# A two-layer gated attention kernel on one core: the first weights centred on TensorE, the first inputs prepared ahead, five staging buffers

## The chip, the cores and the metric

One Trainium2 (trn2) chip, one core. The metric is the device time of one execution in microseconds, as the median over runs. PE is TensorE (PEld its weight loads), DVE VectorE, ACT ScalarE, POOL GpSimd, SP the queue that issues most transfers. A transfer is issued by an engine's queue in its program order; every engine runs its instructions in order and waits where an operand isn't ready.

## The reference

A residual stream x of 16 batches x 128 tokens x 256 passes four blocks; the first is the one around which the change lies:

```python
x = x + tanh(g_xattn[0]) * L0_xattn(layernorm(x), ctx, ...)
x = x + tanh(g_ffn[0])   * L0_ffn(layernorm(x), ...)
x = x + tanh(g_xattn[1]) * L1_xattn(layernorm(x), ctx, ctx, ...)
x = x + tanh(g_ffn[1])   * L1_ffn(layernorm(x), ...)

# L0_xattn: 16 heads of 128, 8 key/value groups
ln_out = _ln(hidden_states, ln_w, ln_b)
q  = _ln(_fp8_linear_pertensor(ln_out, wq, wq_scale, q_in_scale).reshape(b, s, g, hpg, d), qln_w, qln_b)
k  = _ln(_fp8_linear_pertensor(ln_out, wk, wk_scale, k_in_scale).reshape(b, s, g, d), kln_w, kln_b)
v  = _fp8_linear_pertensor(ln_out, wv, wv_scale, v_in_scale).reshape(b, s, g, d)
core = _gqa(q, k, v)
qx = _ln(_fp8_linear_pertensor(ln_out, wqx, ...), qxln_w, qxln_b)
kx, vx = split(cond @ w_kv_x.T);  kx = _ln(kx, kxln_w, kxln_b)
xout = _gqa(qx, kx, vx)
cat = concatenate([core, xout]);  catq = _div_clamp_fp8(cat, proj_smooth)
return einsum(catq, wproj) * (proj_in_scale * proj_w_scale)
```

Queries and keys are layer-normalised over the 128 elements of a head. The mean that this subtracts can be taken out of the weights instead: when each head's 128 output columns of the weight matrix have zero mean (per input row), the projected head has zero mean. This is called centring here.

## The kernel before

The first block is 32 units: units 0 to 15 are one batch each of self-attention, units 16 to 31 one batch each of cross-attention. A unit goes through: preparation of its input (`prep_norm` subtracts and scales on DVE to xh; `prep_tr` transposes on PE and applies ln_w, ln_b on DVE to lnT; `prep_scale` multiplies on POOL to in_y; `prep_round` clamps and rounds on DVE; `prep_last` ends the rounding on POOL to xs and xx, and writes xx to memory, xqx), projection in eight blocks of 512 columns (L431: K 0 and 1, Q 2 to 5, V 6 and 7), eviction on ACT to raw or vt (L443, L440), statistics on DVE (`bn`, L452), a reciprocal root (q_r, L312), its multiplication into raw on POOL (`mult`, L475), transposes of the heads (L486) with eviction on ACT to kT, qT (L495), scores (L504), maximum on DVE (mx, L512), exponentials on ACT (L520), division on POOL (L532), transposes (L540), values (L550), smoothing and rounding to cat (L561, L237), and the output product (L591).

The loop runs over steps n from -11; a unit takes four steps, and at each step `do` and `once` call the stages of several units at their lags, so that stages of different units interleave. `front` gives the two projection blocks of a step: unit u is projected from n = 4u - 5. The order of the calls gives priorities; a scheduler with a cost model of its own settles the order on each engine.

The weights are loaded in the same loop, by `loads`: keys and queries at n = -8, -6 and -5, values at -4, projection weights (`load_proj`, wproj) at -2 and -1. `load_split` loads a 128x512 tile into a staging buffer (`stage`, three buffers), centres it for K and Q (`center`: a reduce and a scaling on DVE, L212 and L213, a subtraction on POOL, L214), and splits it into a rounded part on ACT (L202) and the rest on DVE (L203). `load_proj` splits without centring (L199, L200). `stats` loads four batches of x (xg) and takes their statistics. `load_kv1` loads small weights of the third block (ak, av) and a tile of ctx, and `kv1` (L640, L644) uses them. The weights for the cross half come into the same staging buffers at n around 56 to 60 (`load_kvx`, `load_split` with K_QX).

Where the input preparation stands in a step, before: 

```python
            once(n, -6, "prep_last")
...
            once(n, -8, "prep_norm")
            once(n, -8, "prep_tr")
            once(n, -7, "prep_scale")
            once(n, -7, "prep_round")
```

Of the kernel before, what the change touches and what calls it, by code (L numbers as in the profile page):

```python
# [9 lines left out]
F32 = mybir.dt.float32  # L10
# [5 lines left out]
ALU = mybir.AluOpType  # L16
AX = mybir.AxisListType

P = 128
B = 16  # L20
DM = 256
# [10 lines left out]
K_Q, K_K, K_V, K_QX = 0, 1, 2, 3  # L32
# [3 lines left out]
def flamingo_kernel(  # L36
# [27 lines left out]
    nc = tc.nc  # L64
# [6 lines left out]
    const = ctx.enter_context(tc.tile_pool(name="const", bufs=1))  # L71
# [11 lines left out]
    def ps_tr(shape):  # L83
        return ps("tr", shape, 2)
# [17 lines left out]
    def stay_after(ins, other):  # L102

        tc.add_manual_dep(
            ins.ins, other.ins.name,
            mybir.DependencyInfo(
                mybir.DependencyClass.NoSync, mybir.DependencyReason.DATA
            ),
            reason="the other is awaited",
        )  # L110

    def kpn(ap):
        return ap.rearrange("(k p) n -> p k n", p=P)
# [7 lines left out]
    ident = const.tile([P, P], F32, name="ident")  # L121
# [45 lines left out]
    NST = 512  # L167
# [39 lines left out]
    def center(st, dst):  # L207

        nh = NST // P
        sh = st.rearrange("p (h d) -> p h d", d=P)  # L210
        mean = small.tile([P, nh], F32, tag="wmean", name="wmean")
        nc.vector.tensor_reduce(mean, sh, AX.X, ALU.add)  # L212
        nc.vector.tensor_scalar(mean, mean, 1.0 / P, None, ALU.mult)  # L213
        nc.gpsimd.tensor_tensor(  # L214
            dst.rearrange("p (h d) -> p h d", d=P), sh,
            mean[:, :, None].to_broadcast([P, nh, P]), ALU.subtract,
        )

    def e4m3(dsts, y, pool):


        n = y.shape[1]
        e = pool.tile([P, n], BF16, tag="e8_e", name="e8_e")
        t = pool.tile([P, n], BF16, tag="e8_t", name="e8_t")
        nc.vector.tensor_scalar(y, y, FP8_MAX, -FP8_MAX, ALU.min, ALU.max)
        nc.vector.tensor_scalar(
            e.bitcast(U16), y.bitcast(U16), 0x7F80, None, ALU.bitwise_and
        )

        nc.vector.tensor_scalar(e, e, 2.0**-6, 24.0, ALU.max, ALU.mult)  # L230
        nc.vector.tensor_tensor(t, y, e, ALU.add)  # L231

        def last(other=None):
            at = 0
            for dst in dsts:
                part = slice(at, at + dst.shape[1])
                ins = nc.gpsimd.tensor_tensor(dst, t[:, part], e[:, part], ALU.subtract)  # L237
                if other is not None:
                    stay_after(ins, other)
                at += dst.shape[1]  # L240

        return last
# [11 lines left out]
    with (  # L254
# [3 lines left out]

        wt = {}
        wpr = {}  # L260

        def load_split(kind, src, c):

            for k in range(KD):
                st = ap.tile([P, NST], F32, tag="stage", name="stage", bufs=3)
                nc.sync.dma_start(
                    out=st, in_=src[k * P : (k + 1) * P, c * NST : (c + 1) * NST]
                )
                scale = wsc[:, 2 * kind + k : 2 * kind + k + 1]
                if kind != K_V:  # L270
                    center(st, st)
                slot = "q" if kind == K_QX else "qkv"[kind]
                hi, lo = (
                    (xp if i and slot != "q" else wp).tile(
                        [P, NST], F32R, tag=f"w{slot}{i}{k}{c}", name=f"w{slot}{i}{k}{c}"
                    )
                    for i in range(2)
                )
                split(st, scale, hi, lo)
                wt[kind, 0, k, c], wt[kind, 1, k, c] = hi, lo  # L280
# [11 lines left out]
        def load_proj(cross, q):  # L292

            n = NST // DM
            dst = wp.tile([P, 4, 2, DM], F32R, tag=f"wp{q}", name=f"wp{q}")
            for c in range(0, 4, n):
                h0 = 16 * cross + 4 * q + c
                st = ap.tile([P, n, DM], F32, tag="stage", name="stage", bufs=3)
                nc.sync.dma_start(out=st, in_=kpn(wprojT)[:, h0 : h0 + n, :])
                split(st, None, dst[:, c : c + n, 0, :], dst[:, c : c + n, 1, :])  # L300
            wpr[cross, q] = dst
# [15 lines left out]
        def stats(g):  # L317

            xg = ap.tile([P, 4, DM], F32, tag="xg", name="xg", bufs=1)
            nc.sync.dma_start(  # L320
                out=xg, in_=x_in[4 * g : 4 * g + 4].rearrange("b s d -> s b d")
            )
            mv = small.tile([P, 4, 2], F32, tag="mv0", name="mv0", bufs=2)
            for j in range(4):
                stx = small.tile([P, 6], F32, tag="st0", name="st0")
                nc.vector.bn_stats(stx, xg[:, j, :])
                nc.vector.bn_aggr(mv[:, j, :], stx)

            v = small.tile([P, 4], F32, tag="v1", name="v1", bufs=1)
            nc.vector.tensor_scalar(v, mv[:, :, 1], 1.0 + EPS, EPS * EPS, ALU.mult, ALU.add)  # L330
            rr = rsqrt0(v, 4, "x")
            for j in range(4):
                norms[4 * g + j] = (xg[:, j, :], mv[:, j, 0:1], rr[:, j : j + 1])
# [278 lines left out]
        units = [Unit(u) for u in range(NU)]  # L612
# [3 lines left out]
        av = ap.tile([P, KD, NG * HD], F32, tag="av", name="av", bufs=1)  # L616
        cxs = {}
# [2 lines left out]
        kv1_at[4 * (B - 1) + 1] = B - 1  # L620

        def load_kv1(b):
            if b == 0:
                for k in range(KD):
                    nc.sync.dma_start(
                        out=ak[:, k].rearrange("p (g d) -> p g d", d=HD),
                        in_=akT[k * P : (k + 1) * P, :].rearrange(
                            "p (g h d) -> p g h d", h=NH // NG, d=HD
                        )[:, :, 0, :],
                    )  # L630
                nc.sync.dma_start(out=av, in_=kpn(avT))
            cxs[b] = ap.tile([P, KD, P], F32, tag="ctx", name="ctx")
            nc.sync.dma_start(out=cxs[b], in_=kpn(ctxT)[:, :, b * P : (b + 1) * P])

        def kv1(b):
            cx = cxs.pop(b)
# [42 lines left out]
        def once(n, step, name, *args):  # L679

            m = n - step
            if m % 4 == 0 and 0 <= m // 4 < NU:
                getattr(units[m // 4], name)(*args)
# [7 lines left out]
        first, last = -11, 4 * NU + 7  # L691
        for n in range(first, last + 1):
            for m in range(0, B, 4):
                if n == 4 * m - 11:
                    stats(m // 4)
            once(n, -8, "load")
            for f, args in loads.get(n, ()):
                f(*args)
            ab = [front(n, i) for i in range(2)]
            do(n, 1, "recip")  # L700
            do(n, 4, "quant_last")
            do(n, 1, "divide")
            do(n, 0, "scores")
            do(n, 2, "probs")
            do(n, 0, "top")
            do(n, 0, "exp")
            if ab[0]:
                ab[0][0].project(ab[0][1])
                ab[0][0].evict(ab[0][1])
            once(n, -6, "prep_last")  # L710
            do(n, 3, "values")
            do(n, 3, "smooth")
            if ab[0]:
                ab[0][0].bn(ab[0][1])
            once(n, -2, "rstd")
            for blk in range(2):
                once(n, -2, "mult", blk)
                once(n, -1, "heads", blk)
            do(n, -2, "mult_q")
            do(n, -1, "heads_q")  # L720
            do(n, 3, "quant")
            if ab[1]:
                ab[1][0].project(ab[1][1])
                ab[1][0].evict(ab[1][1])
                ab[1][0].bn(ab[1][1])
            if n + 4 in kv1_at:
                load_kv1(kv1_at[n + 4])
            if n in kv1_at:
                kv1(kv1_at[n])
            do(n, 5, "output")  # L730
            once(n, 8, "residual")
            once(n, -8, "prep_norm")
            once(n, -8, "prep_tr")
            once(n, -7, "prep_scale")
            once(n, -7, "prep_round")

    G = 4
    NT = G * P
# [85 lines left out]
    for j in range(B):  # L824
# [9 lines left out]
        out=before, in_=ones, pattern=[[1, P]], compare_op=ALU.is_gt, fill=0.0,  # L834
# [20 lines left out]
    def route(b0, G):  # L855
# [88 lines left out]
        out=causal, in_=causal, pattern=[[-1, P]], compare_op=ALU.is_ge, fill=NEG,  # L944
# [5 lines left out]
    for q in range(P // 32):  # L950
# [3 lines left out]
            out=rows, in_=rows, pattern=[[-HD, NQ]], compare_op=ALU.is_ge, fill=0.0,  # L954
# [3 lines left out]
            out=rows, in_=rows, pattern=[[HD, NQ]], compare_op=ALU.is_ge, fill=0.0,  # L958
# [223 lines left out]
    ap = f2.enter_context(tc.tile_pool(name="a1", bufs=2, side="right", reuse_waits="tile"))  # L1182
# [171 lines left out]
```

## Time and profile before

| | us |
|---|---|
| median of 3 runs | 1501.8 (1501.51 to 1504.62) |
| profiled execution, its own time | 1503.01 |
| its span | 1501.3 |
| PE busy | 1369.6 (91%) |
| DVE busy | 988.6 (66%) |
| ACT busy | 838.4 (56%) |
| POOL busy | 687.6 (46%) |
| unit 0's first projection (L431) starts | 26.54 |
| unit 1's | 50.6 |
| unit 2's | 76.0 |

Times in the profile count from the span's start. A line of the timeline has the start, the time taken, the engine, the line of the kernel, the operation, output and input, and in brackets how long the engine stood idle before and what ended that. The clock column (PEclk) is the share of TensorE's full speed that was granted. A matmul of float32 operands is two instructions in the trace.

### The profile page before, as it was taken

Reading aid. Unit: us, or ns where it says so; the run is one execution under the profiler, and the core shown is the slowest. Engines: PE = TensorE matmul, PEld = TensorE weight load, DVE = VectorE, ACT = ScalarE, POOL = GpSimd, SP = SyncE. Lnnn points to the kernel's source line nnn. Section 1 sums busy time; section 2 is a strip of 40 time slices with the busy share of each in tenths; the row PEclk is TensorE's granted clock in tenths of the full one; section 3 lists DMA queues with packets and bytes.
Section 4 is the critical chain, followed back from the end, with each engine's and each line's share of the span. In section 5 each row is a group of like instructions: output and inputs, shape, how many; then the busy total and the mean of one; then the engine's idle time right before and its main releaser. Section 6 shows DMA issues by size and latency. Waiting matters only on the chain. (4 is left out here: it accounts for less than half of the span.)

```text
span 1501.3 us, 21652 instructions
## 1 busy us (share of the span) xinstructions
PE 1369.6 (91%) x6852; PEld 964.4 (64%) x6852; DVE 988.6 (66%) x2597; ACT 838.4 (56%) x2496; POOL 687.6 (46%) x615
## 2 busy tenths in 40 slices
PE   2789899899988999999999997999999999985998
PEld 1578778687776777777777766555544444444887
DVE  7867878778689777777676764453478787762100
ACT  3666566666656676666666663164476575741221
POOL 4476677677766565656556563121032322111111
PEclk9699999999999999999999998899999999986999
DMA  4300101000013100000000000700042212122652
GB/s 133 110 17 23 38 22 38 21 22 27 22 55 104 45 29 19 15 16 17 12 18 15 15 4 27 211 8 14 31 128 53 75 50 63 40 75 76 196 189 70
DMA packets 78770, 80.37 MB, mean 54 GB/s; under 512 B 15291, under 2 KB 64891, under 8 KB 78656
## 3 DMA queue, kind: packets, MB, share of 16 engines
q1 hardware_dynamic: 65152, 55.29, 12.7%
q10 hardware_dynamic: 11456, 17.63, 3.6%
q0 software_dynamic: 2048, 6.07, 1.1%
q8 instruction: 55, 0.90, 0.3%
q14 instruction: 59, 0.48, 0.1%
HBM read 57.14 MB, written 22.05 MB: 53 GB/s over the span
## 5 line engine op out<-in xcount | busy, mean ns | idle before, releaser
L532 POOL TENSOR_TENSOR e<-e,sums 128x512 f32<-128x512 f32 x128 | 141.4, 1105 | 239.7 <-DVE sums L528 100.8
L475 POOL TENSOR_TENSOR raw<-raw,q_r 128x512 f32<-128x512 f32 x192 | 211.3, 1126 | 21.0 <-DVE q_r L312 19.6
L520 ACT ACTIVATE e<-ps_sc,mx 128x128 f32<-128x128 f32 x512 | 181.1, 368 | 63.6 <-DVE mx L512 58.1
L452 DVE BATCH_NORM_STATS2 q_st<-raw 128x6 f32<-128x128 f32 x768 | 174.2, 279 | 64.2 <-ACT raw L443 63.6
L591 PE MATMUL ps_acc<-wp,cat 128*128 128x512 f32 x512 | 159.3, 433 | 14.0 <-POOL cat L237 13.4
L504 PE MATMUL ps_sc<-kT,qT 128*128 128x128 f32 x1024 | 140.9, 281 | 23.9 <-ACT qT L495 23.9
L542 ACT COPY eT<-ps_tr 128x512 f32<-128x512 f32 x128 | 75.3, 588 | 156.3 <-PE ps_tr L540 156.3
L504 PEld LDWEIGHTS ps_sc<-kT,qT 128*128 128x128 f32 x1024 | 132.4, 194 | 44.1 <-ACT qT L495 36.6
L237 POOL TENSOR_TENSOR cat<-e_t,e_e 128x1024 fp32r<-128x1024 bf16 x64 | 136.6, 2135 | 43.5 <-DVE e_t L231 43.5
L1082 ACT ACTIVATE e<-ps_sc,mx 128x128 f32<-128x128 f32 x512 | 139.0, 392 | 30.5 <-DVE mx L1073 30.1
L550 PE MATMUL ps_pv<-eT,vt 128*128 128x256 f32 x512 | 133.8, 383 | 1.0 <-DVE cat_y L561 1.0
L443 ACT COPY raw<-ps_mm 128x512 f32<-128x512 f32 x192 | 113.8, 593 | 29.2 <-PE ps_mm L431 25.8
L591 PEld LDWEIGHTS ps_acc<-wp,cat 128*128 128x128 f32 x512 | 94.6, 191 | 53.4 <-POOL cat L237 20.1
L486 PE MATMUL ps_tr<-ident,raw 128*128 128x128 f32 x768 | 115.2, 276 | 13.6 <-POOL raw L475 11.6
L486 PEld LDWEIGHTS ps_tr<-ident,raw 128*128 128x128 f32 x768 | 91.6, 141 | 47.5 <-POOL raw L475 20.5
L561 DVE TENSOR_TENSOR cat_y<-ps_pv,r_sm 128x512 bf16<-128x512 f32 x128 | 87.1, 680 | 47.2 <-PE ps_pv L550 46.7
L550 PEld LDWEIGHTS ps_pv<-eT,vt 128*128 128x128 f32 x512 | 97.3, 192 | 30.9 <-issue 10.5
L512 DVE TENSOR_REDUCE mx<-ps_sc 128x4 f32<-128x512 f32 x128 | 87.2, 682 | 38.5 <-PE ps_sc L504 37.8
L495 ACT ACTIVATE qT<-ps_tr,hv 128x512 f32<-128x512 f32 x128 | 101.2, 791 | 19.9 <-PE ps_tr L486 17.7
L520 ACT ACTIVATION_READ_ACCUMULATOR e<-ps_sc,mx 128x1 f32 x512 | 105.4, 206 | 0.0
L1093 PEld LDWEIGHTS ps_tr<-ident,e 128*128 128x128 f32 x512 | 59.9, 142 | 64.9 <-ACT e L1082 28.1
L1073 DVE TENSOR_REDUCE mx<-ps_sc 128x8 f32<-128x1024 f32 x64 | 77.6, 1212 | 30.2 <-PE ps_sc L1066 20.9
(221 smaller groups left out, 2687.0 us busy)
## 6 DMA issues: line engine op xcount, KB each, us to landing
w1t<-in_w ACTq DMA_DIRECT2D x8, 1024.0 KB
w2t<-in_w ACTq DMA_DIRECT2D x8, 1024.0 KB
disp<-empty SPq DMA_DIRECT2D x16, 257.0 KB
xe<-disp SPq DMA_DIRECT2D x8, 514.0 KB
ctx<-in_ctxT SPq DMA_DIRECT2D x32, 128.0 KB
stage<-in_wprojT SPq DMA_DIRECT2D x16, 256.0 KB
ods<-og SPq DMA_DIRECT2D x128, 32.0 KB
ov<-ods SPq DMA_DIRECT2D x32, 128.0 KB
```

Source lines behind the costliest of these rows:

```text
L237: ins = nc.gpsimd.tensor_tensor(dst, t[:, part], e[:, part], ALU.subtract)
L443: nc.scalar.copy(raw.rearrange("p h d -> p (h d)"), pm)
L452: nc.vector.bn_stats(self.st[:, 4 * blk + j, :], self.raws[blk][:, j, :])
L475: ins = nc.gpsimd.tensor_tensor(src, src, self.r[:, 4 * blk : 4 * blk + 4, None].to_broadcast([P, 4, P]), ALU.mult,)
L486: nc.tensor.transpose(pt[:, j, :], src[:, j, :], ident)
L495: nc.scalar.activation(dst, pt, AF.Identity, scale=hv[:, col : col + 1], bias=hv[:, col + 1 : col + 2])
L504: nc.tensor.matmul(pscore[:, j, :], qT[:, j, :], self.kT[:, 2 * c + j // 2, :], start=True, stop=True,)
L520: nc.scalar.activation(e[:, j, :], pscore[:, j, :], AF.Exp, bias=self.mx[:, j : j + 1], accum_out=sums[:, j : j + 1],)
L532: nc.gpsimd.tensor_tensor(e, e, sums[:, :, None].to_broadcast([P, 4, P]), ALU.mult)
L550: nc.tensor.matmul(pv[:, 2 * g : 2 * g + 2, :], self.vt[:, gg * P : (gg + 1) * P], eT[:, 2 * g : 2 * g + 2, :], start=True, stop=True,)
L591: nc.tensor.matmul(self.acc, self.cat[c // 2][:, h % 8, :], wpr[self.cross, c][:, j, :, :], start=(h == 0), stop=(h == 15),)
L1082: nc.scalar.activation(e[:, i, :], s[:, i // NQ, i % NQ, :], AF.Exp, bias=mx[:, i : i + 1])
```

## The change

Three things. The key and query weights of the self-attention half (12 tiles) are no longer centred by `center` but by `centered`: a tile is transposed on PE in four 128x128 pieces, copied out of PSUM (on ACT for the first half of the input rows, on DVE for the second), and multiplied by cen = identity - 1/128, which gives the centred tile in PSUM; the split reads it there. The staging buffers are five instead of three, at both places. Unit 0's input is prepared at the first step, n = -11, before any weight is loaded. The transfers of ak, av and the first ctx are ordered after the last load that `load_split` has issued by then (`stay_after`: an order on the queue, no wait).

```diff
+    cen = const.tile([P, P], F32, name="cen")
+    nc.gpsimd.memset(cen, -1.0 / P)
+    nc.gpsimd.tensor_tensor(cen, cen, ident, ALU.add)
+
+    def centered(st, t, k, pc):
+
+        nh = NST // P
+        pt = ps_tr([P, nh, P])
+        for h in range(nh):
+            nc.tensor.transpose(pt[:, h, :], st[:, h * P : (h + 1) * P], ident)
+        if k:
+            nc.vector.tensor_copy(t, pt)
+        else:
+            nc.scalar.copy(t, pt)
+        for h in range(nh):
+            nc.tensor.matmul(
+                pc[:, h * P : (h + 1) * P], t[:, h, :], cen, start=True, stop=True
+            )
+        return pc
...
+        staged = {}
...
-                st = ap.tile([P, NST], F32, tag="stage", name="stage", bufs=3)
-                nc.sync.dma_start(
+                st = ap.tile([P, NST], F32, tag="stage", name="stage", bufs=5)
+                staged["last"] = nc.sync.dma_start(
                     out=st, in_=src[k * P : (k + 1) * P, c * NST : (c + 1) * NST]
                 )
                 scale = wsc[:, 2 * kind + k : 2 * kind + k + 1]
-                if kind != K_V:
+                if kind == K_QX:
                     center(st, st)
+                elif kind != K_V:
+
+                    t = ap.tile([P, 4, P], F32, tag="e", name="stageT", bufs=3)
+                    st = centered(st, t, k, (ps_sc if c % 2 else ps_mm)([P, NST]))
...
-                st = ap.tile([P, n, DM], F32, tag="stage", name="stage", bufs=3)
+                st = ap.tile([P, n, DM], F32, tag="stage", name="stage", bufs=5)
...
         def load_kv1(b):
+            behind = lambda ins: stay_after(ins, staged["last"]) if b == 0 else None
             if b == 0:
                 for k in range(KD):
-                    nc.sync.dma_start(
+                    behind(nc.sync.dma_start(
...
-                nc.sync.dma_start(out=av, in_=kpn(avT))
+                behind(nc.sync.dma_start(out=av, in_=kpn(avT)))
             cxs[b] = ap.tile([P, KD, P], F32, tag="ctx", name="ctx")
-            nc.sync.dma_start(out=cxs[b], in_=kpn(ctxT)[:, :, b * P : (b + 1) * P])
+            behind(nc.sync.dma_start(out=cxs[b], in_=kpn(ctxT)[:, :, b * P : (b + 1) * P]))
...
+            if n == first:
+                for name in ("prep_norm", "prep_tr", "prep_scale", "prep_round", "prep_last"):
+                    getattr(units[0], name)()
...
-            once(n, -6, "prep_last")
+            if n > -6:
+                once(n, -6, "prep_last")
...
-            once(n, -8, "prep_norm")
-            once(n, -8, "prep_tr")
-            once(n, -7, "prep_scale")
-            once(n, -7, "prep_round")
+            if n > -7:
+                once(n, -8, "prep_norm")
+                once(n, -8, "prep_tr")
+                once(n, -7, "prep_scale")
+                once(n, -7, "prep_round")
```

More of the change, by code (lines that the diff above doesn't have):

```diff
@@ L629, in load_kv1 @@
                         )[:, :, 0, :],
-                    )
-                nc.sync.dma_start(out=av, in_=kpn(avT))
+                    ))
+                behind(nc.sync.dma_start(out=av, in_=kpn(avT)))
             cxs[b] = ap.tile([P, KD, P], F32, tag="ctx", name="ctx")
-            nc.sync.dma_start(out=cxs[b], in_=kpn(ctxT)[:, :, b * P : (b + 1) * P])
+            behind(nc.sync.dma_start(out=cxs[b], in_=kpn(ctxT)[:, :, b * P : (b + 1) * P]))
         def kv1(b):
```

## The prediction

> **What bounds the kernel now.** I read the busy table by stretches first, to see where TensorE is the limit and where it isn't (columns: stretch, length, busy PE, PEld, DVE, ACT, POOL, clock, DMA share, GB/s).
>
> ```profile
> 0.00:40.00 40.00, 10.15 (x23) 6.32 (x23) 32.10 (x80) 12.76 (x20) 19.49 (x21) 0.98 0.42 126
> 40.00:80.00 40.00, 31.96 (x129) 22.35 (x129) 34.64 (x99) 26.36 (x68) 20.68 (x17) 0.72 0.36 106
> 440.00:480.00 40.00, 30.89 (x146) 23.28 (x146) 37.08 (x85) 23.40 (x64) 28.07 (x24) 0.91 0.30 91
> 520.00:560.00 40.00, 38.22 (x198) 27.90 (x197) 30.41 (x78) 27.20 (x77) 26.22 (x21) 1.00 0.13 37
> ```
>
> In the first 80 us DVE leads (67 of 80) and PE has 42; from 80 to 440 PE has about 36.7 of 40, from 480 to 880 over 38. So time taken out of the first 80 us or out of 440:480 stays out. Then the timeline of POOL and DVE, for what lets a unit begin:
>
> ```profile
> 48.48 2.10 POOL L237 TENSOR_TENSOR xs<-e_t,e_e 128x768 fp32r<-128x768 bf16 x1 [6.11 <-DVE e_t L231]
> 53.40 0.16 DVE L312 SCALAR_TENSOR_TENSOR q_r<-q_a,ps_sc 128x24 f32<-128x24 f32 x1
> 53.64 7.38 POOL L475 TENSOR_TENSOR raw<-raw,q_r 128x512 f32<-128x512 f32 x6 [2.43 <-DVE q_r L312]
> 65.36 1.94 DVE L200 TENSOR_TENSOR wp<-stage,wp 128x512 fp32r<-128x512 f32 x1
> 73.43 0.68 DVE L231 TENSOR_TENSOR e_t<-in_y,e_e 128x1024 bf16<-128x1024 bf16 x1
> 74.26 1.69 POOL L237 TENSOR_TENSOR xs<-e_t,e_e 128x768 fp32r<-128x768 bf16 x1 [3.71 <-DVE q_dif L459]
> ```
>
> xs releases a unit's projections: unit 0 at 26.5, unit 1 at 50.6, unit 2 at 76.0 us, then 99.9 and 128.6. From the first q_r to unit 2's xs is 22.4 us (53.56 to 75.95), through which DVE is full; seven of the eight projection splits (L200) lie in it. PE around the hand-over to the second half:
>
> ```profile
> 470.00 2.04 POOL L214 TENSOR_TENSOR stage<-stage,wmean 128x512 f32<-128x512 f32 x2
> 471.99 2.56 POOL L237 TENSOR_TENSOR cat<-e_t,e_e 128x1024 fp32r<-128x1024 bf16 x1
> 474.61 1.21 PE L591 MATMUL ps_acc<-wp,cat 128*128 128x512 f32 x4 [3.32 <-POOL cat L237]
> ```
>
> Last the clock, in windows laid on its own changes (columns: stretch, length, busy PE, clock):
>
> ```profile
> 48.99:52.41 3.42, 3.00 (x6) 0.50 0.37 108
> 52.41:55.82 3.41, 3.16 (x8) 0.50 0.55 164
> 55.82:59.23 3.41, 3.32 (x23) 1.00 0.42 85
> 103.61:107.02 3.41, 1.57 (x10) 1.00 0.00 0
> 107.02:110.43 3.41, 3.41 (x13) 0.50 0.00 0
> ```
>
> A window of 3.00 us busy left the clock at half, one of 3.16 or more raised it, one of 1.57 lowered it. The 1.00 before 38.7 us is no reading: at 26.5 eight matmuls took 3.78 us, the pace of half speed.
>
> **The change part by part.** In the compiled order the engines differ only in the first 80 us and around 440:480; between and after it is the same, so I cost these two places.
>
> Taken out: 12 reduces (L212, 671 ns), 12 scalings (L213, about 150) and 12 POOL subtractions (L214, 1126): 10 us of DVE, 13.4 of POOL. Put in: 48 transposes and 48 products on PE, 6 copies each on ACT and DVE. Near rows: four transposes start 0.77 us before what follows at half clock (68.25) and 0.36 at full (112.56); four products like L504's take 1.70 (70.88 to 72.58) and 0.89 (111.67 to 112.56). A copy on ACT is L443's 0.58. No DVE copy out of PSUM is shown: 0.41 (L225, SBUF) is the low bound, 0.91 (L203's mean, stretched beside POOL) the high one; L512 reads the same PSUM tile in 0.68, which I take. Per pair of tiles PE needs 4.9 us at half clock and 2.5 at full; ACT 0.58 + 2 x 0.72 = 2.0; DVE 0.68 + 2 x 0.75 = 2.2. PE sets the pace; the products' ps_mm and ps_sc are free until unit 0, and stageT's buffers (tag e) until the first exponentials at 62. At full clock a pair also waits for the first copy (0.4 + 0.1 + 0.68 before the first product, then 1.78): 3.0 us.
>
> x: it lands at 6.0 as before. Without the reduces between, v is at 7.9 (8.88), xh at 9.5 (14.1), the transposes at 9.7, lnT 11.1, in_y 13.0; four DVE steps (0.66, 0.41, 0.41, 0.68) and one copy between make 16.0; xs 2.09 more: 18.1, 8.4 us earlier. It is no longer what PE waits for.
>
> Weights: PE begins them at 10.2. Tile 0 at half clock until 13.4; tile 1's copy is queued on DVE behind the rounding, to 15.5, an idle of 1 us; tiles 1 and 2 end at 18.6. From 15.5 PE is full, so the first whole window raises the clock between 19 and 22.4; I take 20.5. Tiles 3 to 10 end at 31.5. SP holds tile 8 behind xqx, which waits for xx (19.0); it lands by 21.5 and is needed at 24, so that costs nothing; a tile takes some 2.2 us from issue.
>
> Here a rule speaks against the change. In the trace the window 107.02:110.43 held four transposes (107.95 to 108.93, over a quarter of it), was busy throughout, and raised the clock, though one at 88% did not. The Trainium skill (TensorE: Matmul & The Clock Gate, Part 4: PE-mode transpose) says that transposes don't count as PE-busy the same way for the full clock. By the rule only two thirds of the centring would count and it all runs at half: tile 10 ends at 38 to 40. By the row, 31.5. I go by the row; the rule is the rival below.
>
> Unit 0: K at 32, Q and V to 42.7, paced by ACT's queue (0.58 eviction + 0.62 projection cast = 1.2 a block; the casts wait for projection weights, which SP now issues behind ak, 1.6 us, av, 2.62, and ctx: 0.4 us lost). Unit 1's xh is transposed only among these, and its lnT stands on DVE behind four blocks of statistics (16 x 0.28): 40.5 to 41.5. in_y 43.5; then clamp and rounding with three L200 splits between (2.2 + 2.1): 48; xs 50.1, against 50.6. So nearly all of the lead is lost here, and PE idles 7 us and falls to half clock, as before it also was.
>
> The first q_r stands behind all eight splits now, and the last three wait for transfers whose buffers the first splits free (issue 45.2 to 47.4, 2.6 us to land, a cast each): 52.7, against 53.56. What has been won by then is five to seven splits of 0.7 us or more that are no longer ahead of unit 2. After q_r DVE has 13 us of queue up to unit 2's e_t instead of 20. Chain: first heads and score 7 us, mx, statistics, lnT to 62.6 to 63.3, in_y to 65.3, then DVE's rounding among other rows to 69.5, xs 71.4 against 75.95. Taken: 4.5 us earlier; bounds 0 (chain slips behind ACT) and 8.
>
> Hand-over (440:480): the query weights of the second half stage in five buffers instead of three, so five tiles lie ready and not three. In the order q_r goes ahead of a weight split that waited for ACT (466.76 becomes about 465.2), and on POOL one subtraction and one e leave the stretch ahead of cat: cat ends at 471.8 instead of 474.55. PE resumes 2.7 us sooner, and the half-clock window after that stall (475 to 478.4, worth 1.7) may go. Against that, e now stands behind cat. Bounds -1 and 4.5; I take 3.
>
> At nothing: ak, av and ctx issued later (first read at 78.9, ctx lands before 45), xb earlier, cen's making on POOL (under 1 us before 3 us, needed at 12): if that cover went, each would cost its own issue, 0.5 to 2.6 us.
>
> Sum: -4.5 - 3 = -7.5 us. The profiled run took 1503.0 (span 1501.3 plus 1.7), 1.2 above the median of 1501.8; taking the same off the median gives 1494.3.
>
> **The rivals.** Only the hand-over pays: unit 2 waits for POOL and ACT, not DVE, and begins near 76 as now. For it: unit 1's xs gains only half a us. Against: L200 rows fill DVE at 60 to 67. Time 1498.8. The chance is 0.2.
>
> The clock stays at half through the centring, as the rule has it. Tile 10 ends 8 us later, unit 0's blocks at 1.86 instead of 1.2 add 3, unit 1's lnT comes 11 later, xs at 61, q_r near 63, unit 2's xs at 81.5: +5.5, with the hand-over's gain 1504.3, without it 1507.3. It decides if no window of the centring reaches 93% busy as the clock counts it; for it the rule and the 1 us idle at 14.5, against it 107.02:110.43. Chance 0.12.
>
> That the change doesn't do what it says: the inputs do come first, but the first matmul waits for the weights' centring, so "first" buys nothing by itself; this is inside the first two cases.
>
> **How the numbers follow.** Likeliest, 0.68: 1494.3, from 1488 to 1499. With the rivals the range is 1488 to 1503.5, leaving out the worse half of the clock case and a tail below. The measurement tells about 0.2% (3 us) from no change. Faster: 0.63 of the first case and 0.09 of the second, 0.72; slower: half of the clock case and mishaps, 0.1; same 0.18.
>
> **What would show it.** Right: unit 0's xs near 18, centring products ending at 31 to 33 with the clock at full from about 20, unit 1's K near 50, first q_r near 53, unit 2's K at 70 to 73, the wait for cat at 472 gone. Wrong: products four in 1.7 us past 25, unit 1's K after 55, unit 2's K at 76 or more, a new wait for e after 470.

## The result and the profile after

| us | before | after |
|---|---|---|
| median of 6 runs each | 1502.98 (1501.51 to 1506.25) | 1493.39 (1491.31 to 1497.49) |
| profiled span | 1501.3 | 1491.4 |

The ratio is 0.9936, with a 95% interval of 0.9919 to 0.9953: 9.6 us less, beside a forecast of 1494.3 us.

The busy table by stretches of the kernel after (stretch, length, then busy PE, PEld, DVE, ACT, POOL with counts, clock, DMA share, GB/s):

```profile
0.00:40.00 40.00, 26.82 (x172) 22.51 (x172) 25.48 (x72) 21.56 (x36) 5.58 (x11) 1.00 0.58 172
40.00:80.00 40.00, 29.66 (x163) 22.55 (x163) 30.84 (x97) 25.13 (x72) 26.22 (x22) 0.91 0.26 78
440.00:480.00 40.00, 33.30 (x179) 25.82 (x178) 36.63 (x96) 25.92 (x75) 27.76 (x22) 0.98 0.33 101
520.00:560.00 40.00, 38.09 (x205) 29.77 (x206) 30.19 (x85) 28.04 (x81) 23.00 (x19) 1.00 0.05 15
```

DVE falls from 67 us to 56 in the first 80, PE rises from 42 to 56 (the centring is PE work now), and the middle of the second half is as it was. PE's timeline shows the order of the start:

```profile
10.30 0.66 PE L401 MATMUL ps_tr<-ident,xh 128*128 128x128 f32 x2 [10.30 <-DVE xh L392]
22.49 1.16 PE L235 MATMUL ps_mm<-cen,stageT 128*128 128x128 f32 x8 [0.40 <-DVE stageT L231]
32.41 1.69 PE L457 MATMUL ps_mm<-wk,xs 128*128 128x512 f32 x6
48.96 3.74 PE L457 MATMUL ps_mm<-wk,xs 128*128 128x512 f32 x8 [6.43 <-POOL xs L258]
68.77 0.73 PE L457 MATMUL ps_mm<-wk,xs 128*128 128x512 f32 x2 [1.25 <-POOL xs L258]
```

PE does nothing for 10.3 us and then begins with the input, not with the weights. The three L457 rows are the first keys of units 0, 1 and 2: 32.4, 49.0 and 68.8 us, where before they were at 26.5, 50.6 and 76.0. Unit 0 is later and unit 2 is 7.2 us earlier. What releases units 1 and 2, on DVE and POOL:

```profile
50.07 1.28 DVE L200 TENSOR_TENSOR wp<-stage,wp 128x512 fp32r<-128x512 f32 x2
51.98 0.15 DVE L338 SCALAR_TENSOR_TENSOR q_r<-q_a,ps_sc 128x24 f32<-128x24 f32 x1
```

```profile
16.47 1.65 POOL L258 TENSOR_TENSOR xs<-e_t,e_e 128x768 fp32r<-128x768 bf16 x1 [2.66 <-DVE e_t L252]
46.04 2.87 POOL L258 TENSOR_TENSOR xs<-e_t,e_e 128x768 fp32r<-128x768 bf16 x1 [3.62 <-DVE e_t L252]
67.07 1.65 POOL L258 TENSOR_TENSOR xs<-e_t,e_e 128x768 fp32r<-128x768 bf16 x1 [3.19 <-DVE sums L554]
```

All eight projection splits (L200) stand ahead of q_r, and from the end of q_r to the end of unit 2's xs it takes 16.6 us (52.13 to 68.72); before, from 53.56 to 75.95, it took 22.4.

To follow the gain through the kernel I take the same instruction in both profiled executions: the first output product of a unit (after minus before).

| | shift, us | added there |
|---|---|---|
| unit 4 | -5.6 | the start |
| unit 12 | -5.7 | |
| unit 14 | -7.5 | the hand-over to the second half |
| unit 28 | -7.8 | |
| last matmul | -9.9 | behind the changed places |

### The profile page after: what moved, and what is told of

Same layout as the page of the kernel before. It is cut to its first block, busy times and chain, and to the rows that moved or that the text cites. A ratio compares the mean times of both kernels' runs of the same rounds, so it can differ in the third digit from the quotient of the medians.

```text
span 1491.4 us, 21918 instructions
## 1 busy us (share of the span) xinstructions
PE 1373.6 (92%) x6996; PEld 970.9 (65%) x6996; DVE 977.2 (66%) x2579; ACT 843.0 (57%) x2502; POOL 673.3 (45%) x605
## 5 line engine op out<-in xcount | busy, mean ns | idle before, releaser
L512 PEld LDWEIGHTS ps_tr<-ident,raw 128*128 128x128 f32 x768 | 91.5, 141 | 50.1 <-POOL raw L501 22.3
L576 PEld LDWEIGHTS ps_pv<-eT,vt 128*128 128x128 f32 x512 | 96.2, 190 | 31.0 <-issue 10.9
L521 ACT ACTIVATE qT<-ps_tr,hv 128x512 f32<-128x512 f32 x128 | 101.4, 792 | 19.0 <-PE ps_tr L512 16.8
```

The source lines that it names most:

```text
L512: nc.tensor.transpose(pt[:, j, :], src[:, j, :], ident)
L521: nc.scalar.activation(dst, pt, AF.Identity, scale=hv[:, col : col + 1], bias=hv[:, col + 1 : col + 2])
L576: nc.tensor.matmul(pv[:, 2 * g : 2 * g + 2, :], self.vt[:, gg * P : (gg + 1) * P], eT[:, 2 * g : 2 * g + 2, :], start=True, stop=True,)
```

## The experiments

Twelve kernels, each timed against before on the same chip, with five or six runs each. In the table "start" is the shift of unit 4's first output product against before, "hand-over" what is added between units 12 and 14, "rest" what is added between unit 28 and the last matmul, all from one profiled execution each, in us. The last column is the ratio of times.

| | start | hand-over | rest | median us (before, timed beside it) | ratio, 95% |
|---|---|---|---|---|---|
| after | -5.6 | -1.8 | -2.1 | 1493.39 (1502.98) | 0.9936 [0.9919, 0.9953] |
| e1 after, 3 buffers | -4.5 | -0.2 | -0.8 | 1496.95 (1502.81) | 0.9961 [0.9948, 0.9973] |
| e2 before + products | -4.7 | -0.1 | +0.2 | 1496.55 (1502.81) | 0.9952 [0.9938, 0.9966] |
| e3 after, no products | -4.9 | -1.5 | +0.1 | 1497.11 (1502.81) | 0.9963 [0.9951, 0.9975] |
| e4 before + 5 buffers | -4.8 | -1.8 | +1.1 | 1496.57 (1502.81) | 0.9959 [0.9944, 0.9974] |
| e5 before + products + 5 buffers | -7.8 | -1.9 | -1.8 | 1490.28 (1500.76) | 0.9929 [0.9912, 0.9946] |
| e6 after, unit 1 early too | -7.6 | -1.2 | -6.0 | 1492.01 (1500.76) | 0.9939 [0.9921, 0.9958] |
| e7 after, warm-up, with waits | -5.1 | -1.8 | -0.7 | 1494.33 (1500.76) | 0.9955 [0.9940, 0.9970] |
| e8 after, 6 buffers | -8.1 | -1.5 | -3.1 | 1491.89 (1500.76) | 0.9944 [0.9927, 0.9960] |
| e9 after, no input-first | -7.0 | -1.8 | -2.6 | 1491.09 (1500.99) | 0.9935 [0.9921, 0.9948] |
| e10 before + products + 6 buffers | -7.9 | -1.2 | +1.5 | 1490.18 (1500.99) | 0.9925 [0.9912, 0.9939] |
| e11 as e10, unit 1 early | -13.4 | -1.8 | -3.0 | 1487.91 (1500.99) | 0.9919 [0.9906, 0.9933] |
| e12 after, dense warm-up | -6.9 | -1.6 | +2.6 | 1495.24 (1500.99) | 0.9956 [0.9943, 0.9970] |

The start and the hand-over belong to the change. The rest doesn't: behind the hand-over every engine has the same instructions in the same order as in before, in all of these kernels, and it still ranges from -6.0 to +2.6. For that reason the verdicts below go by the first two columns, and the times, whose intervals overlap, are only the second witness.

The start column holds two pieces of chance as well. Every kernel but e8 and e11 loses time near 100 us, where PE waits some 2 us for the heads of a unit and the clock then falls to half for 3.4 us. The wait is the same 2.4 us in after and in e8, but the clock's window lies otherwise over it. PE alone in after and then in e8, in the window in which the wait ends (stretch, length, busy PE, clock):

```profile
96.89:100.30 3.41, 1.02 (x6) 1.00 0.00 0
97.12:100.53 3.41, 1.71 (x11) 1.00 0.00 0
```

The clock falls behind the first and stays full behind the second. That is worth 1.3 us: ahead of it e8 is 1.2 us in front of after (the first transposes behind the wait start at 98.48 and 99.67), at unit 4 2.5. The other piece is the input x. In the traced execution of after it lands late:

```profile
6.65 0.43 DVE L352 BATCH_NORM_STATS2 st<-xg 128x6 f32<-128x256 f32 x1 [1.01 <-DMA xg<-in_x]
```

In twelve of the other thirteen this row starts between 6.03 and 6.26 (in e2 at 6.48). PE begins with x in after, so up to 0.6 us of what after lies behind another kernel can be this and not the change.

**Which part makes the gain: e1 to e4.**

e1: `-  bufs=5` `+  bufs=3` at both places of after. 

> The changed kernel with three staging buffers instead of five. Theory: the start is set by the products and by DVE's queue, not by staging, so unit 2's K still begins near 69 us (before 76.0, changed 68.8); the hand-over after 440 us goes back to its old order, with PE waiting some 3.3 us for cat, and some 2 us of the gain are lost: ratio to before about 0.995 to 0.996. Rival (the deeper staging is what pays at the start): unit 2's K at 74 or later, ratio 0.998 or more.

e2: before, with `centered` for K and Q and nothing else. 

> The kernel before with the products alone (three buffers, unit 0's input where it was, small transfers where they were). Theory: the products take 10 us of reduces off DVE and 13 us off POOL, and that alone moves unit 2's K to 69 to 71 us; nothing is gained at the hand-over: ratio 0.995 to 0.9965. Rival (input first is what pays): unit 2's K at 74 or later, ratio 0.998 or more.

e3: `-  if kind == K_QX:` `+  if kind != K_V:` in after, so that the old `center` does it. 

> The changed kernel with its key and query weights centred on DVE and POOL as before (input first, five buffers, small transfers behind stay). Theory: unit 0's xs comes early (under 20 us) but its weights do not, DVE is full to 67 us as before, unit 2's K at 74 to 77; the hand-over keeps its gain of 2: ratio 0.998 to 0.999. Rival (input first pays): unit 2's K at 71 or earlier, ratio 0.996 or less.

e4: `-  bufs=3` `+  bufs=5` in before. 

> The kernel before with five staging buffers and nothing else. Theory: unit 2's K stays at 75 to 77 us; at the hand-over cat comes earlier and PE waits for it under 2.2 us instead of 3.3, worth 2 us in all: ratio 0.998 to 0.999. Rival (the hand-over's gain in the changed kernel came from the clock's windows, not from the buffers): the shift at the hand-over is under 0.5 us, ratio 1.000.

The hand-over is settled: five buffers give it (e3 and e4: 1.5 and 1.8), three do not (e1 and e2: 0.2 at most), whatever else is in the kernel. At the start e2 came out as its theory had it, with unit 2's keys at 70.99; e1 lost more than its theory allowed (71.14 instead of near 69), and e3 and e4 gained where nothing was expected. The products alone give 4.7 us, but five buffers alone, with the old centring in place, give 4.8 as well. DVE in e4:

```profile
51.87 1.28 DVE L200 TENSOR_TENSOR wp<-stage,wp 128x512 fp32r<-128x512 f32 x2
53.78 0.16 DVE L312 SCALAR_TENSOR_TENSOR q_r<-q_a,ps_sc 128x24 f32<-128x24 f32 x1
```

and in e1, which has the products and three buffers:

```profile
50.37 0.17 DVE L338 SCALAR_TENSOR_TENSOR q_r<-q_a,ps_sc 128x24 f32<-128x24 f32 x1
50.46 0.69 DVE L200 TENSOR_TENSOR wp<-stage,wp 128x512 fp32r<-128x512 f32 x1
55.57 2.47 DVE L200 TENSOR_TENSOR wp<-stage,wp 128x512 fp32r<-128x512 f32 x2 [0.50 <-ACT wp L199]
```

These are two different gains that end at the same unit. With the products q_r comes 3 us earlier than before (50.4 in e1 and 50.0 in e2, against 53.4), and five splits stand ahead of it where before had one, but three are still behind it. With the buffers q_r comes as late as before (53.8), but no split is behind it: the eight run from 44.6 to 53.1, where in before they ran from 51.8 to 67.3. In e4 unit 2's first keys start at 70.64, in e1 at 71.14, in before at 76.00. e3 is e4 with the other two parts added, and its start is the same (4.9): without the products they buy nothing.

**Whether they add up, and what the other parts do: e5 and e9.**

e5: e2 and e4 together, without input-first and without the transfers behind the weights. 

> The kernel before with the products and the five buffers, without the other two parts: unit 0's input stays where it was and the small transfers stay before the weights. Theory: products and buffers each bring all eight projection splits, or most, ahead of unit 2, so their gains at the start overlap; the other two parts buy nothing, since unit 0's xs isn't what PE waits for. Unit 2's K at 68.5 to 70 us, the hand-over as in the changed kernel, ratio to before 0.993 to 0.995, the changed kernel's. Rival (the input first and the transfers behind give the 0.8 us by which the changed kernel's fifth unit is ahead of the one-part kernels, or more): unit 2's K at 70.5 or later, ratio 0.9955 or more.

e9: after without its input-first part, `-  if n == first: ... units[0]` and the two conditions. 

> The kernel after without its input-first part: unit 0 is prepared at its old place in the loop, after the first weights; products, five buffers and the small transfers behind the weights stay. Products and five buffers alone moved unit 4's first output product 7.8 us earlier than before, the whole change only 5.6, so one of the two other parts costs about 2.2 us. If it is input-first (TensorE runs in order and its first matmul waits for the input at 10.3 us, while the weights are there at 7.15): TensorE starts at about 7.2, unit 0's keys at 30.6, unit 2's at 66.4, unit 4 is 7.5 to 8 us earlier than before and the time is about 1491. If it is the transfers behind the weights: TensorE also starts at 7.2, but the projection weights come later, unit 2's keys stay at 68.5 to 69, unit 4 gains 5 to 6 and the time is about 1494.

Together, products and buffers give 7.8 us of the 9.5 that their single gains add up to. (At unit 2's keys it is 9.6 of 10.4: 66.39 us in e5.) So the whole change, at 5.6, loses 2.2 us to its other two parts, up to 0.6 of it perhaps the late x. PE in e9:

```profile
7.17 1.94 PE L229 MATMUL ps_tr<-ident,stage 128*128 128x128 f32 x8 [7.17 <-DMA stage<-in_wkT]
30.73 1.18 PE L457 MATMUL ps_mm<-wk,xs 128*128 128x512 f32 x4
47.53 3.73 PE L457 MATMUL ps_mm<-wk,xs 128*128 128x512 f32 x8 [6.67 <-POOL xs L258]
67.32 0.73 PE L457 MATMUL ps_mm<-wk,xs 128*128 128x512 f32 x2 [1.25 <-POOL xs L258]
```

The weights are there at 7.17, and the input's transposes only at 10.30. Standing first in PE's order, they hold 3.1 us of ready work. In e9, where the weights go first, these three units start 1.4 to 1.7 us earlier than in after, and the start gains 7.0. So input-first costs 1.4 us between these two executions, and 0.8 if all of after's late x is taken out; the medians don't show it (after 9.6 below before, e9 9.9). The remaining 0.8, e9 against e5 (0.5 at unit 12), is the small transfers behind the weights. SP's queue in both shows where: in e5 ak, av and ctx are issued from 4.8 to 10.9 us, ahead of weights whose buffers aren't free yet; in e9 they lie from 28.5 to 34.0 between the projection weights. There a cast on ACT waits for its projection weight, which in e5 it does not (it starts at 35.71):

```profile
36.62 0.62 ACT L199 CAST wp<-stage 128x512 fp32r<-128x512 f32 x1 [0.85 <-DMA stage<-in_wprojT]
```

The evictions of unit 0's queries stand behind it on ACT, their statistics and unit 1's second lnT behind these on DVE (38.55 instead of 37.69), and from there all is 0.87 later, q_r too (50.55 instead of 49.68). Neither theory of e9 had the loss divided.

**How far buffers and preparation reach: e6, e8, e10, e11.**

e6: `-  getattr(units[0], name)()` `+  ` the same for units 0 and 1 at the first step of after. 

> The changed kernel with unit 1's input prepared at the first step too. Theory (the lead is lost because unit 1's lnT stands on DVE behind unit 0's statistics): PE goes from unit 0's V straight to unit 1's K at 42 to 44 us instead of 49, its 6 us of idling and the half clock after it go, the first q_r comes at 48 to 50, and unit 2's K at 64 to 67: 2 to 4 us more gained, ratio to before 0.991 to 0.9925. Rival (the first q_r, behind the eight projection splits on DVE, is what sets unit 2, not unit 1's input): unit 1's K early, but unit 2's K still at 68 to 69, ratio as the changed kernel's, 0.9935 to 0.9945.

e8: `-  bufs=5` `+  bufs=6` in after. 

> The changed kernel with six staging buffers. Theory for the hand-over: a buffer more puts one more query weight ahead, but PE's wait for cat there is by now POOL's own queue (three multiplications and a subtraction), so at most 0.5 us more; at the start, splits are all ahead of q_r already: unit 2's K within 0.7 us of 68.8. Ratio as the changed kernel's, 0.9925 to 0.995. Rival (every buffer shortens the hand-over in proportion, 0.9 us each): ratio 0.9925 or less and another 1 us at the hand-over.

e10: `-  bufs=5` `+  bufs=6` in e5. 

> The kernel before with the products and six staging buffers, no input-first, no transfers behind. The whole change with six buffers gained 8.1 us at unit 4 where five gave 5.6; products with five buffers alone gained 7.8. If what the sixth buffer gives and what dropping input-first gives are separate, unit 4 is about 10 us earlier than before, unit 2's keys start at about 64.5 and the time is about 1488. If both only fill the same slack (they buy the same earlier projection weights on VectorE ahead of unit 2), it is 8 to 8.5 earlier and about 1490.5, as with five.

e11: e10, with unit 1's preparation at n = -6, behind unit 0's last step, instead of n = -4 to -2. 

> As the one with products and six staging buffers, and unit 1's input is prepared two steps earlier (in the step of unit 0's first projection, behind unit 0's). Nothing else moves. TensorE then has unit 1's input when unit 0's values end, so that its idle of 6 to 7 us goes and unit 1's keys start at about 41 to 42. If unit 2 then waits for the same VectorE and ScalarE work as in the kernel with two units prepared at the first step (keys of unit 1 at 43.1, of unit 2 at 65.7), half of the 6 us or less arrives: unit 2's keys at about 64, unit 4 is 9 to 10.5 us earlier than before, time about 1488. If all of it arrives, unit 2's keys come at 60 and the time is about 1484. If VectorE bounds the whole start (its queue to unit 2's input is as long as before), unit 2 stays at 66 and the time at 1490.

The sixth buffer gives 2.5 us in after (e8) and nothing in e5 (e10, 0.1). But 1.3 of the 2.5 is the clock that did not fall, up to 0.6 of the rest after's late x, and unit 2's keys start no earlier (69.09, after 68.77), as e8's theory had it. So how much the sixth buffer itself gives in after is open, between 0.6 and 1.2 us. At the hand-over it adds nothing (1.5 and 1.2). At about -8 something else holds, and e11 shows what. PE in e11:

```profile
40.90 2.10 PE L454 MATMUL ps_mm<-wk,xs 128*128 128x512 f32 x8
62.79 0.73 PE L454 MATMUL ps_mm<-wk,xs 128*128 128x512 f32 x2 [2.15 <-POOL xs L257]
```

DVE in e11:

```profile
46.31 0.16 DVE L335 SCALAR_TENSOR_TENSOR q_r<-q_a,ps_sc 128x24 f32<-128x24 f32 x1
```

Unit 1's keys start without a wait as unit 0's values end, at 40.9 instead of 46.9 (e10); the idle of 6 us ahead of them is gone (one of 2 us stays, ahead of unit 2); q_r is 3.4 us earlier, unit 2's keys 4.4, unit 4's output product 5.5. The last 1.5 of this 5.5 goes with the clock that did not fall near 100 us; ahead of that place e11 leads e10 by 4.1 (93.16 and 97.21). So the wait for unit 1's xs was the next bound. That is more than the half I had expected. e6 tried the same with unit 1 prepared at the very first step: PE then gets to its first weight still later (at 11.25 us, after at 10.76, and the clock rises at 17.1 instead of 15.0), and only 2.0 us of gain over after is left. e11 is the version to take: 1487.9 us, 13.1 below the before that was timed beside it, where after was 9.6 below its own and e10 10.8. The intervals of the ratio overlap, so the times alone don't decide it; but of the start, 13.4 against 5.6, the two pieces of chance explain 2.1 us at most.

**The clock: e7 and e12.**

e7: 36 transposes of the identity ahead of after's first matmul, four to a PSUM tile. 

> The changed kernel with 36 transposes of the identity into an unused PSUM tile put ahead of everything on PE, where it idles until x arrives (1.8 to 9.5 us). It asks whether transposes alone raise the clock. If they count as work (as the window 107 to 110 us of the kernel before suggests), the clock is full from 5 to 9 us, unit 0's first four-piece group takes 0.36 to 0.45 us instead of 0.8, and the products of tile 0 0.9 instead of 1.84; the time changes by under 2 us, because DVE holds tile 1. If they don't (the rule of the page), the clock stays at half until the products have run, as in the changed kernel until 15.

e12: the same, all into one PSUM tile. 

> The kernel after, with 36 transposes of the identity ahead of its first matmul as in the earlier run, but all into one PSUM tile, so that no wait for PSUM lies between them (in the earlier run groups of four waited for it, and the clock rose in the third all-transpose window, at 12.4 us, not in the first two). Their result is not used. If transposes count as busy for the clock and the waits were what broke the earlier windows, the clock is full within 3.4 to 7 us of the first transpose, at 5 to 9 us, and the 36 take under 10.5 us (421 ns a piece at half clock, about 210 at full). If transposes count only in part (the Trainium skill, TensorE: Matmul & The Clock Gate), it rises no earlier than at 12 us again. Unit 4's first output product: 5 to 6 us earlier than before in both cases, time about 1494.

The forecast had weighed a rule of the Trainium skill (TensorE: Matmul & The Clock Gate, Part 4), by which transposes don't count for the full clock, against one window of before. In after the clock is full from 14.97; the windows on PE alone (stretch, length, busy PE, clock):

```profile
11.56:14.97 3.41, 3.41 (x16) 1.00 0.24 77
45.69:49.10 3.41, 0.14 (x1) 0.50 0.76 232
49.10:52.52 3.42, 3.42 (x8) 0.50 0.40 94
```

The full window 11.56:14.97 raised it, although eight of its sixteen instructions were transposes and its products filled only 1.84 us of it (12.59 to 14.43). An idle window (42.28 to 45.69 held 0.25 us of work) lowered it for unit 1's first keys, and the full one from 49.10 raised it again. The 1.00 shown before 14.97 is again no reading. e7 left the matter half open: its records fill 95% or more of the windows, but the starts show four transposes some 0.213 us apart and then 0.27 us of idle; the clock rose only behind the third window, at 12.4. With one PSUM tile (e12) there is no such idle. Its transposes alone (the tile ps_pv):

```profile
1.54:4.49 2.95, 2.95 (x14) 1.00 0.43 90
4.49:7.10 2.61, 2.61 (x24) 1.00 1.07 333
```

The first fourteen start 213 ns apart, up to 4.37 us, the other twenty-two 109 ns apart, from 4.54 on (x24 counts two records that reach over from the row above): nothing but transposes had run, and the clock doubled. (The 421 ns a piece that I had put for half clock is the length of a record, not the distance of the starts.) In this kernel, for 128x128 transposes of float32, the rule does not hold. The start gains 6.9 us instead of 5.6, where I had expected no change. That the centring begins at full clock is a part of it at most: x's statistics begin 0.54 us earlier in this execution (6.11 against 6.65), as they do in most of the kernels without a warm-up. The time of 1495.24, 5.8 below before, does not show the gain, and e7's, 6.4 below, is no better; what these two kernels lose against after's 9.6 stays open.

## Why the prediction was right, and where it wasn't

- x: xs was forecast to end at 18.1 and ended at 18.12 (16.47 + 1.65). That it is so close is luck: x was put at 6.0 and came at 6.65, so the chain behind it took 0.6 us less than forecast (in e8 and e1 xs ends near 17.5). The DVE copy out of PSUM, taken at 0.68 between bounds of 0.41 and 0.91, took 0.68.
- Centring: a pair of tiles took 3.32 us, not 3.0, but the clock was full at 14.97, not 20.5. Tile 1's copy did come as late as forecast (15.1 to 15.8), but PE was full ahead of it, with tile 0's products and the next transposes, so the window up to 14.97 counted already; the idle behind it was 0.45 us, not 1. The two errors nearly cancel, which is luck: the end was forecast at 31.5 and came at 32.1. The rival of the half clock fell, by after's windows and by e12.
- Units 1 and 2: unit 1's xs ended at 48.9 (forecast 50.1), q_r ended at 52.13 (52.7), unit 2's xs at 68.7 (71.4). The mis-sized term is the stretch behind q_r, "After q_r DVE has 13 us of queue up to unit 2's e_t instead of 20" and the chain built on it: 18.7 us were forecast from q_r to the end of unit 2's xs and 16.6 were measured. DVE had 10.3 us of work there, within 14.1. (In before it was not full either, as I had read it: 16.8 busy of 19.9 up to e_t.) The difference stands at lnT already, which ended at 60.8 and not at 62.6 to 63.3; from there to xs it took 7.9 us, and 8.1 or more were forecast. So 4.5 was too small: 7.2 at unit 2, of which 5.6 were left at unit 4.
- Which part does it: I priced the products as ten us off DVE and took the order "all eight splits ahead of q_r" as part of the same story. e1, e2 and e4 show that the products bring five of the eight ahead and only the buffers all of them, and that the buffers alone are worth as much at the start as the products alone. The sum was right in sign without this, but a reader of the forecast would have taken the buffers for a matter of the hand-over, and without them the start loses 1.1 us in this change (e1) and 3.1 where it is products and buffers alone (e2 against e5).
- "'First' buys nothing by itself": it costs 0.8 to 1.4 us (e9), because PE's first place in order went to an operand that was usable 3.1 us after the weights. The forecast had the 10.2 us at which PE begins, and did not ask when it could have begun.
- The small transfers, set "at nothing", cost 0.8 (e9 against e5); the 0.4 that the text gave for the issue of ak, av and ctx among the projection weights was the right mechanism, a cast that waits for its projection weight, at half its size.
- Hand-over: 3 was forecast, 1.8 came. PE there, first a row of before and then two of after, and POOL in after:

```profile
459.95 0.66 PE L540 MATMUL ps_tr<-ident,e 128*128 128x128 f32 x4 [1.27 <-POOL e L532]
455.99 0.66 PE L566 MATMUL ps_tr<-ident,e 128*128 128x128 f32 x4 [2.09 <-POOL e L558]
467.20 1.20 PE L617 MATMUL ps_acc<-wp,cat 128*128 128x512 f32 x4 [1.98 <-POOL cat L258]
```

```profile
452.01 2.49 POOL L214 TENSOR_TENSOR stage<-stage,wmean 128x512 f32<-128x512 f32 x2 [0.70 <-DVE wmean L213]
454.46 1.48 POOL L558 TENSOR_TENSOR e<-e,sums 128x512 f32<-128x512 f32 x1
464.04 1.04 POOL L214 TENSOR_TENSOR stage<-stage,wmean 128x512 f32<-128x512 f32 x1
465.04 2.11 POOL L258 TENSOR_TENSOR cat<-e_t,e_e 128x1024 fp32r<-128x1024 bf16 x1
```

  As forecast, one subtraction and one e left the stretch ahead of cat, and the wait for cat fell from 3.32 to 1.98 us. It did not go: with the start's shift of 5.7 taken out, cat ends at 472.8 and not at 471.8. The subtraction that was moved forward now stands ahead of an earlier e (four of them behind the e before it, where before had three), and PE's wait for that e grew from 1.27 us to 2.09 (in e3 and e4 to 2.10). The rival "only the hand-over pays" fell with e1 and e2, which have no hand-over and most of the start (4.5 and 4.7 of 5.6).
- The total: 5.7 + 1.8 + 0.3 = 7.8 us up to unit 28, against 7.5 forecast; the median moved by 9.6. That the sum fits is partly luck, for the start was 1.2 us more than forecast and the hand-over 1.2 less. The rest lies where nothing was changed and where thirteen kernels scatter over 8.6 us in single executions. It goes with the clock: behind unit 28 it stood at half for 64.9 us in before, 54.6 in after, 47.8 in e6 (rest -6.0) and 71.7 in e10 (+1.5), and over the fourteen executions the two have a correlation of 0.89, with 0.32 us of time for each us at half. No run sets these windows, so that they are the cause is argued and not shown.

## What to carry to other kernels

Ask of every reordering which engine's queue gets a new first entry, and when that entry's operand is ready: what is loaded first isn't what should be issued first. A staging pool's depth sets the order of work on other engines, so price it at the start as well as where the profile shows it waiting, and run each part of a change alone, since gains that end at one unit need not add up. Before parts are priced finer than 1 or 2 us from one execution each, look for chance in them: here the landing of the first input (0.6 us) and one window of the clock (1.3 to 1.5). When a start has been shortened, look for the next releaser (here unit 1's xs) before adding more of what helped.

## What the runs showed of the hardware

Transposes alone raised TensorE's clock to full within 2.95 us of the first one (e12), after which they started every 109 ns instead of every 213.

How much idle a window may hold before the clock stays at half can be read from the starts, not from the records' lengths, which cover short waits. Counted here is what an instruction takes in an unbroken row at half clock, 0.213 us for a transpose and 0.427 for a product of 512 columns. e7's window from 5.58 to 8.99, with three idles of 0.27 us, comes to 72%, and before's from 48.99 to 52.41 to 72% as well: both left the clock at half, though their records fill 95% and 88%. e7's from 8.99 to 12.41 comes to 81%, before's from 52.41 to 55.82 to 82%, e12's from 1.08 to 4.49 to 85%: all three raised it. In e10 a window at 75% raised it (47.45 to 50.87, records 81%) and another at 75% did not (890.54 to 893.95). So in these windows the border lies near 75%, with or without transposes, and this count does not make it sharper.
